# Tokens laid out as 56 rows by 56: the first and last transform as four 64 by 64 products, the row sums on VectorE

## The chip, the cores and the metric

The kernel runs on one core of a Trainium2 chip. The metric is the device time of one launch in microseconds (us), the median of three runs. A profile of one execution is there beside it; its engines are PE (TensorE's products; PEld is its loading of weights), DVE (VectorE), ACT (ScalarE), POOL (GpSimd) and SP (SyncE, which issues nearly all transfers).

## What is computed

The input is 32 images of 56 by 56 places with 96 channels, all float32. The reference, cut to what matters:

```python
def reference(x, ...):
    # layer 0: LayerNorm over channels, 96 -> 192 product (first half used), 3x3 convolution 192 -> 96
    mu, var = mean(x, -1), mean((x - mu)**2, -1)
    h = (x - mu) * rsqrt(var + 1e-5) * ln_w + ln_b
    x1, _ = split(h @ w_in + b_in, 2)
    x = x + silu(conv3x3(x1, conv_w, 'SAME') + conv_b)
    # layer 1, attention part: t is (32, 3136, 96)
    t = x.reshape(32, 3136, 96)
    h = relu(bn1(layernorm(t) @ w1.T))                 # 96 -> 192
    X = fft(h, axis=1, norm='ortho')                   # over the 3136 places
    xr = relu(X.real * rd - X.imag * idg + rb)
    xi = relu(X.imag * rd + X.real * idg + ib)
    y = ifft(xr + 1j * xi, axis=1, norm='ortho').real
    t = t + bn2(y @ w2.T)                              # 192 -> 96
    # layer 1, FFN with float8 (e5m2) operands: 96 -> 384 -> 96
    h = relu(qlinear(layernorm(t), W1, b1))
    return (t + qlinear(h, W2, b2)).reshape(x.shape)
```

## The kernel before

An image's 3136 tokens lie as 112 partitions (`N1`) by 28 columns (`N2`). `Image` holds the tiles of one image, and each step of it is a small function. Along an image the steps are:

- `fetch` loads x in four chunks of up to 8 columns, `take_in` forms LayerNorm's sums with `stats` (bn_stats on DVE, the power -1/2 on POOL, L147) and scales into `xa` (L410).
- `make_image` calls `image`: TensorE transposes and takes the row sums of a Winograd scheme for four output rows at once, by a product with the table `rows6_sb` (tile `im`, L165). ACT copies it to `img` (L167), the only buffer of its kind; `make_seam` copies two columns between its halves (L418, L419).
- `conv` takes 24 products for each of 9 parts (three groups of 32 output channels by three pairs of planes), tile `cv` (L182 for a part's first product, L186 for the rest). Four of them go to four groups of 32 columns of TensorE's array. `conv_sums` and `conv_silu` combine them on DVE to four output rows each (L203), `to_tokens` transposes back (`st`, L219), `conv_end` adds to the tokens (L439).
- The Fourier transform over 3136 = 112 x 28 is done in two stages. `tokens_a` transposes four columns (`tp_n`, L158), `forth` multiplies by w1 (`ph`, L232; relu on ACT, L235), `forth_a` transforms over the 112 rows (`pa<-h,fa_sb`, L241: 112 by 112, moving 384), and `store_a` writes the result to DRAM (`da`).
- `fetch_a` reads `at` back with the other axis on the partitions. `second` forms the second stage in 28 pages p, in units of eight, eight, eight and four (`px`, L256: for u = 0 and 1 the first 128 channels, for u = 2 the last 64, with the unit's two halves of pages in the two column halves of the array). `second_parts` and `second_relus` apply the filter (L261 to L282). `second_w2` multiplies by w2 (`pg`, L295 and L299), `second_back` goes back through the second stage (`pe`, L309), `store_back` writes `de` to DRAM.
- `fetch_y` reads `y`, `back` transforms back over the rows (`py<-y,ia_sb`, L317), `back_end` adds to the tokens (L516) and forms the third LayerNorm's sums.
- `normal` writes the normalised tokens as float8 (L535 on ACT, L539 on DVE, two columns each), `ffn_start` transposes (L156), `ffn_first` multiplies by W1 (`pf`, L328), `ffn_middle` adds the bias, takes relu (L335) and rounds to float8 (`hq`, L336), `ffn_second` multiplies by W2 (`po`, L342), `ffn_end` adds (L351, L352) and `store` writes out.

The order is a plan by hand. `put(when, step, ...)` in `plan(b)` gives each step of image b a time in eighths of an image's period (8 b + when), the steps are sorted by it and issued so; the scheduler of the language then orders each engine's instructions by priority. About three images are in work at once. `in_turn` keeps loads in program order for the first images.

[...]Tile `a` (two buffers of a bank) holds `tp_n` and `pf`, `q` (two) `im`, `cv` and `st`, `c` (two) `ph`, `px` and `py`, and `b` (two) `pa`, `pg`, `pe` and `po`.

## Time and profile before

| | us |
|---|---|
| median of 3 runs | 3040.65 (3039.39 to 3045.61) |
| span of the profiled execution | 3036.8 |
| PE busy | 2978.4 (98%) |
| PEld busy | 2445.3 (81%) |
| DVE busy | 2348.2 (77%) |
| ACT busy | 2277.4 (75%) |
| POOL busy | 647.5 (21%) |
| mean granted TensorE clock | 0.990 of full |
| largest queue of transfers | 349.24 MB, 43.5% of 16 DMA engines |

A profiled span runs from the first to the last instruction; the median includes what lies around it. A row of the profile names line, engine, operation, tiles (`out<-in`), shape, count, busy time and the mean of one, and then the idle time before its instructions with what ended it. In rows of the timeline the first number is the start in us and the second the time to the last end of the merged instructions. An f32 product is shown as two instructions, a float8 one as one.

### The profile page before, as it was taken

The page shows a single profiled execution, that of the slowest core. Times are in us where ns is not written, and L with a number is a line of the kernel's source. Part 1 is how long each engine was busy: PE and PEld are TensorE (multiplying, and loading weights), DVE is VectorE, ACT ScalarE, POOL GpSimd, SP SyncE. Part 2 cuts the span into 40 slices and gives each one's busy share as a digit, 9 for nine tenths or more (in the row PEclk, how much of TensorE's full clock was granted, in tenths as well). Part 3 has the DMA queues.
Part 4 walks back from the last instruction along what each step waited for, and adds up shares of the span by engine and source line. Part 5 has one row for each costly group of instructions (what it writes and reads, how often), then busy time and mean ns, then how long its engine had stood idle before and what let it go on. Part 6 is the DMA issues. An engine that isn't in the chain of part 4 may idle for free.

```text
span 3036.8 us, 84414 instructions
## 1 busy us (share of the span) xinstructions
PE 2978.4 (98%) x32693; PEld 2445.3 (81%) x32693; DVE 2348.2 (77%) x7248; ACT 2277.4 (75%) x5703; POOL 647.5 (21%) x398
## 2 busy tenths in 40 slices
PE   8999999999999999999999999999999999999997
PEld 7678788888888887888888888888888888888775
DVE  5548777888778887778887778887778887777778
ACT  3467777787777787777787777787777877777877
POOL 2202122222112221122221222221222221121111
PEclk9899999999999999999999999999999999999998
DMA  3533444443454444444444444434444434444443
GB/s 85 144 93 94 117 126 124 118 123 98 121 133 126 117 116 108 122 130 122 123 109 114 125 126 123 127 98 122 124 128 122 123 96 124 129 129 104 113 123 78
DMA packets 495435, 355.37 MB, mean 117 GB/s; under 512 B 329992, under 2 KB 459304, under 8 KB 494808
## 3 DMA queue, kind: packets, MB, share of 16 engines
q1 hardware_dynamic: 493146, 349.24, 43.5%
q8 instruction: 257, 4.21, 0.6%
q10 hardware_dynamic: 1888, 0.74, 0.1%
q14 instruction: 144, 1.18, 0.1%
HBM read 195.73 MB, written 154.14 MB: 115 GB/s over the span
## 4 chain that ended last, share of the span: by engine, by line
PE 88%; DMA 5%; DVE 3%; ACT 2%; issue 1%; POOL 0%; SPq 0%; ACTq 0%; DVEq 0%
PE cv L186 14%; PE ph L232 10%; PE px L256 10%; PE pa L241 9%; PE im L165 7%; PE pe L309 6%; PE pg L299 5%; PE py L317 5%; PE pg L295 5%; PE po L342 4%; PE pf L328 4%; PE cv L182 3%; PE st L219 3%; PE tp_n L158 2%; DMA de<-es 2%; DMA xl<-in_x 1%
## 5 line engine op out<-in xcount | busy, mean ns | idle before, releaser
L186 PE MATMUL cv<-img,wv 97*32 97x196 f32 x13248 | 621.6, 331 | 0.0
L147 POOL TENSOR_TENSOR rs_c<-var_c,mhalf 112x8 f32<-112x8 f32 (+1 forms) x128 | 206.7, 1615 | 1894.1 <-DVE var_c L145 879.1
L186 PEld LDWEIGHTS cv<-img,wv 97*32 97x32 f32 x13248 | 426.8, 109 | 106.9
L235 ACT ACTIVATE h<-ph,rs_b 112x192 f32<-112x192 f32 x896 | 340.1, 449 | 74.1 <-PE ph L232 74.0
L232 PE MATMUL ph<-w1a,n2t 97*112 97x192 f32 x1792 | 381.2, 335 | 2.0 <-ACT n2t L225 0.9
L241 PE MATMUL pa<-h,fa_sb 112*112 112x384 f32 x896 | 372.3, 497 | 0.8 <-ACT h L235 0.8
L330 ACT CAST h<-pf 128x448 f16<-128x448 f32 x672 | 367.5, 567 | 1.1 <-PE pf L328 1.0
L256 PEld LDWEIGHTS px<-fb_sb,at 112*64 112x64 f32 (+1 forms) x3584 | 319.2, 166 | 58.1 <-issue 8.7
L256 PE MATMUL px<-fb_sb,at 112*64 112x112 f32 (+3 forms) x3584 | 353.5, 272 | 8.1 <-DMA at<-da 4.0
L165 PE MATMUL im<-rows_sb,xa 112*97 112x168 f32 x1792 | 321.2, 313 | 2.1 <-DVE xa L410 1.4
L232 PEld LDWEIGHTS ph<-w1a,n2t 97*112 97x112 f32 x1792 | 278.5, 177 | 47.4 <-issue 18.1
L147 POOL TENSOR_TENSOR rs_b<-var_b,mhalf 112x8 f32<-112x8 f32 (+1 forms) x128 | 227.7, 1788 | 397.3 <-DVE var_a L145 310.2
L165 PEld LDWEIGHTS im<-rows_sb,xa 112*97 112x97 f32 x1792 | 264.1, 168 | 33.1 <-issue 15.7
L242 ACT COPY u<-pa 112x384 f32<-112x384 f32 x448 | 226.2, 505 | 75.6 <-PE pa L241 75.4
L272 DVE SCALAR_TENSOR_TENSOR sv<-px,spar_sb,av 128x224 f32<-128x224 f32 (+2 forms) x352 | 152.9, 434 | 151.3 <-ACT av L263 149.8
L336 DVE CAST hq<-h 128x448 fp8e5<-128x448 f16 x672 | 256.1, 386 | 7.5
L335 DVE TENSOR_SCALAR h<-h,b1q 128x448 f16<-128x448 f16 x672 | 220.1, 329 | 40.6 <-ACT h L330 36.1
L299 PE MATMUL pg<-w2x,gt 128*112 128x96 f32 (+1 forms) x1792 | 243.1, 258 | 0.0
L167 ACT COPY img<-im 97x336 f32<-97x336 f32 x448 | 205.5, 461 | 48.6 <-PE im L165 25.8
L299 PEld LDWEIGHTS pg<-w2x,gt 128*112 128x112 f32 (+1 forms) x1792 | 240.8, 178 | 0.0
L261 ACT ACTIVATE av<-px,spar_sb 128x224 f32<-128x224 f32 (+2 forms) x352 | 162.8, 462 | 100.9 <-PE px L256 99.1
L295 PE MATMUL pg<-w2y,gt 128*112 128x192 f32 (+1 forms) x896 | 226.8, 335 | 1.1 <-DVE gt L282 0.7
(121 smaller groups left out, 6197.6 us busy)
## 6 DMA issues: line engine op xcount, KB each, us to landing
da<-u SPq DMA_DIRECT2D x224, 336.0 KB, 3.1
at<-da SPq DMA_DIRECT2D x224, 336.0 KB, 4.2
de<-es SPq DMA_DIRECT2D x448, 84.0 KB, 2.0
y<-de SPq DMA_DIRECT2D x224, 168.0 KB, 2.5
out<-t SPq DMA_DIRECT2D x224, 168.0 KB, 2.6
t<-in_x SPq DMA_DIRECT2D x96, 336.0 KB, 4.4
xl<-in_x SPq DMA_DIRECT2D x93, 336.0 KB, 4.5
t<-in_x SPq DMA_DIRECT2D x32, 168.0 KB, 3.8
```

The source lines that it names most:

```text
L147: nc.gpsimd.tensor_tensor(rs, var, mhalf[:, :n], ALU.pow)
L165: nc.tensor.matmul(ps[:, j], xa[:, j, :], rows6_sb, start=True, stop=True)
L186: tc.keep_in_program_order(nc.tensor.matmul(*args, start=(dx == 0), stop=(dx == 2)))
L232: nc.tensor.matmul(ph[:, j, :], n2t[:, 2 * j2 + j, :], w1a, start=True, stop=True)
L235: nc.scalar.activation(h[:, j], ph[:, j], AF.Relu, scale=rs[:, 2 * j2 + j : 2 * j2 + j + 1])
L241: nc.tensor.matmul(pa, fa_sb, h, start=True, stop=True)
L242: nc.scalar.copy(u[:, 2 * j2 : 2 * j2 + 2, :], pa)
L256: nc.tensor.matmul(px[rows, j], lhs, fb_sb[:, first(p) : first(p + 1)], start=True, stop=True)
L295: nc.tensor.matmul(pg[:, :, j, :], lhs, w2y, start=True, stop=False, skip_group_check=True)
L299: nc.tensor.matmul(pg[:, half, j, :], lhs, w2x, start=False, stop=True, skip_group_check=True)
L330: nc.scalar.copy(h1, pf)
L336: nc.vector.tensor_copy(hq[:, k, :], h2, saturate=False)
```

## The change

Tokens lie as 56 rows on 120 partitions (`NQ`): one half of the image's columns on partitions 0 to 55, the other on 64 to 119, with a gap between. The host lays x out so, and gives it a second time with the channels first (`xc`).

- The row sums are formed on DVE from the channel-first copy: the statistics of a whole image give one power on POOL (`scale`), a transpose on TensorE (`turn`), a write to DRAM, and a read back that spreads the factor over the 96 channel partitions (`fetch_r`). `scaled` multiplies, and `differences`, `ends`, `inner` and `outer` form the six planes of `img`. `image`, `make_seam` and `rows6_sb` are gone.
- The Fourier transform is 56 by 56. `transform_a` and `transform_out` each issue four products of at most 64 by 64 places, at two row groups and two column groups of the array, through `together`.
- `pa`, `px`, `pg`, `pe` and `py` share tile `d`, of two banks, in two buffers. `ph` and `po` go to tile `a`. `second` with u = 0 covers up to eight pages, and its u = 1 is gone; the pages of u = 2 are issued in the order of p.
- All columns of `normal` go to ACT; `hq` is rounded once per group of four columns, to columns padded to 128; several work tiles have one buffer (`m`, `sd`, `av`, `sv`, `gw`, `es`).
- `SHIFT` moves the time of nearly every step, `EARLY` and `WRITE` place the row sums ahead of the convolution, and the scheduler's model of the issue queues is shortened (`short_window`).

The diff, cut to its core:

```diff
-N1, N2 = 112, 28
+N2, NT1 = 28, 112
+HP = 64
+BANK = 512
+NQ = HP + HW
+SHIFT = {
+    "back": 0.002, "back:0": -0.012, "back:1": 0.006, "back:3": 0.047, "back:4": 0.02, "back:5": -0.026,
...
+}
-    def image(xa, b, g, t0):
-
-        ps = psq.tile([C + 1, 2, 2, WC * WG], F32, tag="q", name=f"im_{b}_{g}_{t0}")
-        for j in range(2):
-            nc.tensor.matmul(ps[:, j], xa[:, j, :], rows6_sb, start=True, stop=True)
-        j0 = CT * t0 + g + 1
-        nc.scalar.copy(img[:, :, j0 : j0 + CT + 1 : CT].rearrange("c h j k g -> c j h (k g)"), ps)
+    def together(products):
+
+        for i, (to, lhs, rhs) in enumerate(products):
+            if i == 0:
+                nc.tensor.matmul(to, lhs, rhs, start=True, stop=True)
+                continue
+            with tc.high_priority():
+                tc.keep_in_program_order(nc.tensor.matmul(to, lhs, rhs, start=True, stop=True))
-    def transform_a(h, u, b, g, j2):
-
-        pa = psum2.tile([112, 2, H], F32, tag="b", name=f"pa_{b}_{g}_{j2}")
-        nc.tensor.matmul(pa, fa_sb, h, start=True, stop=True)
-        nc.scalar.copy(u[:, 2 * j2 : 2 * j2 + 2, :], pa)
+    def transform_a(h, u, b, g):
+
+        pa = psum2.tile([128, 2, BANK], F32, tag="d", name=f"pa_{b}_{g}")[:, :, : 2 * H]
+        products = []
+        for c in range(2):
+            for r in range(2):
+                rows = slice(HP * r, HP * r + HW)
+                at = h[rows, 2 * c : 2 * c + 2].rearrange("p j c -> p (j c)")
+                products.append((pa[HP * c : HP * (c + 1), r], fa_sb[rows], at))
+        together(products)
+        nc.scalar.copy(u.rearrange("m r j c -> m r (j c)"), pa)
...
-        n = PG if u < 2 else (p1 - p0) // 2
-        px = psum2.tile([128, n, 2, w], F32, tag="c", name=f"px_{b}_{m}_{u}")
-        for j in range(n):
-            for half in range(1 if u < 2 else 2):
-                p = p0 + u * PG + j if u < 2 else p0 + half * n + j
-                rows = slice(0, 128) if u < 2 else slice(64 * half, 64 * half + 64)
-                lhs = ats[p // PG][:, p % PG, :128] if u < 2 else ats[p // PG][:, p % PG, 128:]
-                nc.tensor.matmul(px[rows, j], lhs, fb_sb[:, first(p) : first(p + 1)], start=True, stop=True)
...
+            for p in range(p0, p1):
+                rows = slice(64 * ((p - p0) // half), 64 * ((p - p0) // half) + 64)
+                at = fb_sb[:, first(p) : first(p + 1)].rearrange("n (r k) -> n r k", r=2)
+                nc.tensor.matmul(to[rows, :, (p - p0) % half, :], ats[p // PG][:, p % PG, 128:], at, start=True, stop=True)
...
-        py = psum2.tile([N1, G4, C], F32, tag="c", name=f"py_{b}_{g}")
-        nc.tensor.matmul(py, ia_sb, y, start=True, stop=True)
-        return py
+        n = min(2, NG - 2 * q)
+        ps = psum2.tile([128, 2, G4, BANK // G4], F32, tag="d", name=f"py_{b}_{q}")[:, :n, :, :C]
+        products = []
+        for h in range(2):
+            for r in range(n):
+                rows = slice(HP * r, HP * r + HW + 1)
+                to = ps[HP * h : HP * (h + 1), r].rearrange("p (i j) c -> p i j c", i=2)
+                products.append((to, ia_sb[rows], y[rows, :, h]))
+        together(products)
...
+    def scaled(im, h):
+
+        a = view(im.xc[h], 0, (LINE // 2, 2 * N2), (WG + 1, 2), (1, WG))
+        r = im.rb[h].rearrange("c (j i g) -> c j i g", i=2, g=WG)
+        nc.vector.tensor_tensor(a, a, r, ALU.mult)
+    def inner(im, h, k):
+
+        x = im.xc[h]
+        b, a = (x[:, :, START[i] : START[i] + WG] for i in (2, 3))
+        nc.vector.tensor_tensor(planes(h, k), a, b, ALU.add if k == 1 else ALU.subtract)
...
-            if j < 2:
+            if j < 4:
                 nc.scalar.activation(
...
         def put(when, f, *args):
+            when += sum(SHIFT.get(key, 0) for key in shifts(f.__name__, args))
             order.append((8 * b + when, len(order), lambda: f(im, *args)))
...
-            at = CONV - 2.485 + 0.531 * i
+            at = CONV - EARLY - 0.35 + 0.531 * i
...
+    EARLY, WRITE = 6.2, 3.5
...
+WINDOW = (1, 1, 2)
```

## The prediction

> **What bounds the kernel now.** I read the busy shares first, then the chain that ended last, then the busy times of the steady stretch from 400 to 2600 us (columns there: length, then busy us and instruction count of PE, PEld, DVE, ACT, POOL; granted clock; DMA share; GB/s), and last the timeline of PE for prices.

> ```profile
> PE 2978.4 (98%) x32693; PEld 2445.3 (81%) x32693; DVE 2348.2 (77%) x7248; ACT 2277.4 (75%) x5703; POOL 647.5 (21%) x398
> ...
> PE 88%; DMA 5%; DVE 3%; ACT 2%; issue 1%; POOL 0%; SPq 0%; ACTq 0%; DVEq 0%
> ```

> ```profile
> 400.00:2600.00 2200.00, 2193.42 (x24430) 1808.53 (x24429) 1746.45 (x5387) 1696.44 (x4262) 490.36 (x288) 1.00 0.45 119
> ```

> PE idles 6.6 us in 2200, at full clock: work taken off PE is time, work put on others is not, until they near PE's period. The stretch holds 24 images (672 ACT copies out of ph, 28 per image): **91.7 us per image**, 32 x 91.7 = 2934, so the remaining 103 us of the 3036.8 us span are ramp and tail.

> Busy means of PE overlap (a 384-column product "takes" 497 ns), so I price by the distance between starts:

> ```profile
> 1506.46 0.36 PE L182 MATMUL cv<-img,wv 97*32 97x196 f32 x1
> 1506.47 0.37 PE L186 MATMUL cv<-img,wv 97*32 97x196 f32 x3
> 1506.66 0.33 PE L182 MATMUL cv<-img,wv 97*32 97x196 f32 x1
> ...
> 1508.49 0.33 PE L182 MATMUL cv<-img,wv 97*32 97x196 f32 x1
> ...
> 1510.48 0.33 PE L182 MATMUL cv<-img,wv 97*32 97x196 f32 x1
> ...
> 1515.41 0.60 PE L219 MATMUL st<-ident,s 128*112 128x128 f32 x4
> 1515.94 0.35 PE L182 MATMUL cv<-img,wv 97*32 97x196 f32 x1
> ...
> 1518.07 0.32 PE L219 MATMUL st<-ident,s 128*112 128x128 f32 x1
> ...
> 1547.04 0.99 PE L256 MATMUL px<-fb_sb,at 112*64 112x112 f32 x16
> 1547.96 0.55 PE L328 MATMUL pf<-n3t,w1q 96*128 96x448 fp8e5 x2
> ...
> 1573.98 0.81 PE L241 MATMUL pa<-h,fa_sb 112*112 112x384 f32 x2
> 1574.62 0.35 PE L328 MATMUL pf<-n3t,w1q 96*128 96x448 fp8e5 x1
> 1574.82 0.73 PE L165 MATMUL im<-rows_sb,xa 112*97 112x168 f32 x4
> 1575.39 0.49 PE L219 MATMUL st<-ident,s 128*112 128x128 f32 x3
> ```

> An f32 product is two records (passes): pa 0.64 us for two passes of 384 columns, im 0.57 for four of 168, both 0.83 to 0.85 ns a column. The convolution's 48 records of 196 columns take 1.99 us: 12 steps of 0.166, each as long as one pass alone, so its four 32-column tiles run side by side. A part before which PE was in another mode takes longer: st x4 to cv is 0.53 where four of st elsewhere take 0.44 (0.09 into tiles), cv to st 2.13 where 1.99 is one part (0.14 out of them).

> [...] Here only column groups are seen overlapping; no row groups occur. [...] L182's second pass starts after three L186 first passes, so a tile's waiting pass doesn't stop the other tiles. [...]

> **The change, part by part, us per image.**
> - *im gone*: 56 records x 0.1425 = **-8.0** on PE; its 14 evacuations and two seams leave ACT (205.5 + 21.5 us in the page and by-form rows, /32 = 7.1), the xa scaling leaves DVE (108.9 / 32 = 3.4).
> - *pa as four 64x64*: 14 products x 0.64 = 9.0 become 7 groups of two steps of 0.32 = 4.5: **-4.5**. *py likewise*: 7 x 0.64 = 4.5 become 4 groups, 2.6: **-1.9**. Row groups are unseen; bounds: four at once as taken; two at once, no gain; one at a time, 0.32 x 56 = 17.9 and 0.32 x 28 = 9.0.
> - *Mode changes*: along PE's compiled order I count 21 per image before and 47 after: 13 more round trips x 0.23 = **+3.0**. A change between two tiled modes is not priced anywhere; taken alike.
> - *px of the last 64 channels*: before, its two column halves alternate, and 16 records take 8 steps (0.92 with the way out). After, four pairs' products go to the lower half and then four to the upper. Nothing shows how far a half runs ahead: 0 if the queue reaches past eight passes, +2.7 if halves never overlap (28 more steps x 0.096). I take an overlap of two passes, as cv holds one pass waiting per tile: 6 + 6 + 6 + 2 steps, **+1.9**.
> - *120 rows instead of 112*: 28 transposes x 8 columns x 0.83 ns = +0.2; the added transpose `turn` +0.1. po's stationary goes from 112 to 128 columns: its 84 starts are 51 ns apart for 96 columns, so weights may bind; bounds -0.7 (43 ns) to +0.5; I take **-0.3** since w1q of 128 columns loads in 103 ns, hq of 112 in 134.
> - PE sum: 91.7 - 8.0 - 4.5 - 1.9 + 3.0 + 1.9 + 0.0 = **82.2**.
> - *Row sums on DVE*: 18 instructions, 12,600 elements. xa gives 549 ns for 384 and 950 for 768: 1.04 ns each, and successive rows overlap by about 80 ns, so about 0.06 fixed: 13.1 + 1.1 = +14.2. Off DVE: xa 3.4; xn wholly to ACT (128.5 / 32 = 4.0); one rounding of hq for three (14 fixed parts, 0.9); fused u 0 and 1 (15 fewer, 1.5); s written in runs of 14, not with stride (526 ns now against 386 of the longer L282): 12 x 0.1 = 1.2. DVE 1746.45 / 24 = 72.8 becomes 72.8 + 14.2 - 11.0 = **76**. ACT: 70.7 - 7.1 + xn 5.7 - 3.5 (fewer, longer copies) = **66**. Both lie under 82, so I price them at nothing, covered by PE; DVE's cover is thin (93%). If PE's products came cheaper still, DVE would be next.
> - *Waits*: DVE is in order, and the sums for the next image wait on `img`, still one buffer, until the convolution has read each plane. Behind them queue the px, py and cv readers, for which PE's two d tiles wait. The bufs=1 tiles (m, sd, av, sv, gw, es) couple engines more. PE idles 0.3 us per image now; I take **1** and bound it by 0 and 6.
> - *Queues*: POOL's four powers become one of 28 columns; from 4 columns (1.1 us) to 8 (1.7 to 2.0), about 5 us: POOL idles 79%. SP issues 57 transfers an image for 50: xc (624 KB x2) and rb (602 KB x2) added, rd twice; rb waits for rd to land, and xl, at, y and out queue behind it. The landing of such transfers is 2 to 4.5 us and they are asked for some 60 us early; bytes rise 22%, the DMA share from 0.45 to about 0.55. Hidden.
> - *Ramp*: image 0 needs all four row statistics (done at 15.3 us now), the power 5, the turn and two transfers 8, then about 10 of row sums before the first convolution: 38 to 40 us instead of 27.3, and im's 8 us of ramp work are gone from that gap. Image 1's sums queue on DVE behind image 0's. +18, bounds +5 and +35. The tail moves normalisation from DVE to ACT: 0.

> Sum: 32 x 83.2 + 103 + 18 = 2783 as span. The runs' median is 3040.65, 3.9 above the profiled span: **2787**.

> **Rivals.** (1) Stalls: the order on paper doesn't hold and PE idles 5 to 6 us an image: 2915 to 2950. For it: DVE at 93%, half the buffers. Against: PE idles 0.3 now at DVE 79%. (2) Row groups don't overlap: pa and py back at 9.0 and 4.5, 88.6 + 1 per image, 2990. (3) *Slower*: tile a paces PE. Its two one-bank tiles served tp_n and pf, 35 uses an image; ph, po and turn make it 57. Measured from first product to end of last copy, ph holds its tile 2.2 us, po 2.2, tp_n 1.9, pf 1.7: 57 x 1.9 / 2 = 54 us. ACT is in order, and a late ACT lengthens each hold; from a mean of 3.2 us the period passes 91.7, and at 3.4 it is 97: 3230. The holds would have to grow by 70% on an engine at 80%, which speaks against it. (4) The four products run one after another, the change not doing what it says: 82.2 + 13.4 + 6.4 = 102 an image, 3390; cv's four tiles speak against it.

> **How the numbers follow.** Main case 0.73 (own range 2690 to 2880: px -0 to +2.7, po, ramp, stall 0 to 3), (1) 0.12, (2) 0.05, (3) 0.06, (4) 0.03, no difference 0.01. Faster 0.90, same 0.01, slower 0.09; 0.2%, 6 us, is about what a measurement here can tell from no change. The range reaches to 2960 to take in the stalls, leaving out 0.05 below and 0.14 above.

> **What would show it.** Right: im gone; pa as eight records whose starts lie in two bunches 0.32 apart; pa to the next product about 0.7 us; PE still over 95% busy; DVE near 76 and ACT near 66 us an image; px of 64 columns in about 14 steps. Wrong: pa's eight records over more than 1.2 us; PE under 93% with waits on DVE or ACT at pa, px or ph; DVE above PE.

## The result, and the profile after

| | before | after |
|---|---|---|
| median, us | 3040.0 (3039.2 to 3045.6) | 3334.8 (3328.0 to 3343.7) |
| ratio | | 1.097 (95% interval 1.095 to 1.099) |
| span of the profiled execution | 3036.8 | 3341.9 |
| mean granted TensorE clock | 0.990 | 0.915 |

The change is slower by 9.7%; the forecast was 2787 in a range from 2690 to 2960. The busy shares and the chain that ended last, from the page of the kernel after:

```profile
PE 2972.6 (89%) x32277; PEld 2191.4 (66%) x32277; DVE 2441.8 (73%) x6128; ACT 2156.7 (65%) x4871; POOL 582.7 (17%) x304
...
PE 44%; DVE 19%; DMA 17%; ACT 10%; issue 3%; SPq 2%; POOL 0%; DVEq 0%; ACTq 0%; POOLq 0%
```

No engine took PE's place: all are less busy than before in share. More than half of the chain lies off PE now (44% PE, 88% before). The stretches by time (columns as in the prediction: length, then busy us and count of PE, PEld, DVE, ACT, POOL, then granted clock, DMA share, GB/s), steady part:

```profile
400.00:2800.00 2400.00, 2189.49 (x24115) 1627.54 (x24115) 1800.33 (x4495) 1607.44 (x3643) 432.97 (x216) 0.93 0.52 134
```

That is 24 images at 100.0 us. PE idles 210.5 us of it, **8.8 us per image**, and the clock of 0.93 is made of stretches at full and at half clock only: about 15% of the time at half. Laid out with the trace's clock records, 100.1 us per image (between the first ph products of images 4 and 28, the first image being 0) are 84.4 us of work at full clock, 8.8 idle and **6.9 lost** because 13.8 us of work ran at half clock. "Work" is the time in which PE has any record, with what ran at half clock counted half. Counted the same way, the kernel before takes 91.9 us per image: 91.6 of work, 0.3 idle, nothing lost. DVE takes 75.0 and ACT 67.0 us after the change.

The four 64 by 64 products, in the timeline of PE (start, us to the last end, engine, line, operation, tiles, shape, count):

```profile
1499.32 0.87 PE L275 MATMUL ph<-w1a,n2t 97*120 97x192 f32 x4
1500.12 0.53 PE L283 MATMUL pa<-h,fa_sb 56*64 56x384 f32 x1
1500.12 0.55 PE L286 MATMUL pa<-h,fa_sb 56*64 56x384 f32 x3
1500.49 0.48 PE L283 MATMUL pa<-h,fa_sb 56*64 56x384 f32 x1
1500.50 0.49 PE L286 MATMUL pa<-h,fa_sb 56*64 56x384 f32 x3
1500.92 0.36 PE L416 MATMUL pf<-n3t,w1q 96*128 96x448 fp8e5 x1
```

All four run at once, in two bunches of four passes 0.37 us apart, and 0.80 us lie from the first to the next product (0.81 in the median of 134 such groups at full clock). So the packing works; the time goes elsewhere. Where a stall ahead of pa comes from is seen in the chain of waits between 1491 and 1512 us (start, us, what):

```profile
1491.38 0.57 DVE t L443
1491.97 3.19 DMA out<-t
...
1495.59 0.55 SPq L447
...
1496.24 3.54 DMA rd<-rt
1499.80 4.34 DMA rb<-rd
...
1504.16 1.79 DVE xc L531
...
1508.15 1.78 DVE xc L531
1509.93 0.36 DVE sv L336
...
1510.53 0.36 DVE sv L337
1510.89 0.37 DVE sv L339
...
1511.31 0.53 PE pa L283
```

Read it downwards: SP stands before the t loads (L447) until an `out` store has landed; rd and rb come behind in its queue and take 3.5 and 4.3 us; VectorE stands at xc until rb is there; the readers of px (L336 to L339) come behind it in its order (px was written by 1503.49 and av, which they read too, by 1506.45; the first of them starts at 1509.85), tile d stays held, and PE waits 2.5 us to write pa.

The wait of SP at the head of this chain is its smallest part. What rd writes out is the copy rt, and that was late itself (two rows of the timeline, of PE and of ACT):

```profile
1493.38 0.27 PE L505 MATMUL tr<-ident,rs_a 120*28 120x120 f32 x1
1495.33 0.23 ACT L507 COPY rt<-tr 28x120 f32<-28x120 f32 x1
```

ScalarE came to rt 1.7 us after the turn, and with rt done at 1495.56 SP held rd only 0.7 us longer (0.7 in the median of images 8 to 27, 2.0 at most). From the end of the turn to rb there are 10.5 us, of which rd and rb take 7.9. And the turn waited for nothing here: PE was not idle ahead of it, and the power that it reads had been ready for 194 us (median, about two images). Its place in PE's order sets when the chain begins.

The list of waits gives the chain in sums (who waited for whom: us in all, times, longest):

```profile
DVE xc L531 <- DMA rb<-rd: 96.3, 41, 8.2
...
PE pa L283 <- DVE sv L339: 58.3, 21, 4.7
```

Of the 8.8 us of idle PE per image, 2.3 end at pa with this release and 1.4 at py when y has landed; the rest is spread over pf (1.6), ph (1.2), po (0.8), cv (0.7) and others. The experiments ask whether this chain is the cause, or one of many.

### The profile page after: what moved, and what is told of

Read it like the earlier page. It is cut to its first block, busy times and chain, and to the rows that moved or that the text cites. A ratio compares the mean times of both kernels' runs of the same rounds, so it can differ in the third digit from the quotient of the medians.

```text
span 3341.9 us, 80656 instructions
## 1 busy us (share of the span) xinstructions
PE 2972.6 (89%) x32277; PEld 2191.4 (66%) x32277; DVE 2441.8 (73%) x6128; ACT 2156.7 (65%) x4871; POOL 582.7 (17%) x304
## 4 chain that ended last, share of the span: by engine, by line
PE 44%; DVE 19%; DMA 17%; ACT 10%; issue 3%; SPq 2%; POOL 0%; DVEq 0%; ACTq 0%; POOLq 0%
PE ph L275 6%; PE cv L228 6%; PE pg L380 4%; PE pg L376 4%; PE px L312 4%; DMA de<-es 3%; PE pe L392 3%; DMA rb<-rd 3%; DMA y<-de 3%; PE pa L283 3%; PE px L320 3%; DMA rd<-rt 3%; PE pf L416 3%; DVE xc L531 2%; ACT xn L687 2%
## 5 line engine op out<-in xcount | busy, mean ns | idle before, releaser
L184 POOL TENSOR_TENSOR rs_c<-var_c,mhalf 120x8 f32<-120x8 f32 (+1 forms) x128 | 220.9, 1726 | 1575.6 <-DVE var_c L182 1562.2
L275 PE MATMUL ph<-w1a,n2t 97*120 97x192 f32 x1792 | 423.0, 362 | 43.0 <-ACT y L438 22.5
L277 ACT ACTIVATE h<-ph,rs_b 120x192 f32<-120x192 f32 x896 | 327.1, 419 | 181.8 <-PE ph L275 180.6
L687 ACT ACTIVATE xn<-t,shift,rs_c 120x96 fp8e5<-120x96 f32 x896 | 367.2, 475 | 43.5 <-DVE shift L681 43.5
L275 PEld LDWEIGHTS ph<-w1a,n2t 97*120 97x120 f32 x1792 | 299.4, 197 | 115.3 <-ACT y L438 31.2
L184 POOL TENSOR_TENSOR rs_b<-var_b,mhalf 120x8 f32<-120x8 f32 (+1 forms) x128 | 206.3, 1614 | 758.9 <-DVE var_b L182 742.2
L416 PE MATMUL pf<-n3t,w1q 96*128 96x448 fp8e5 x672 | 253.0, 391 | 50.9 <-ACT n3t L411 25.8
L283 PE MATMUL pa<-h,fa_sb 56*64 56x384 f32 x448 | 216.8, 567 | 58.3 <-DVE sv L339 58.3
L312 PEld LDWEIGHTS px<-fb_sb,at 112*128 112x128 f32 x1792 | 250.4, 211 | 21.8 <-issue 6.8
L312 PE MATMUL px<-fb_sb,at 112*128 112x112 f32 (+1 forms) x1792 | 256.5, 295 | 9.1 <-DMA at<-da 7.5
L286 PE MATMUL pa<-h,fa_sb 56*64 56x384 f32 x1344 | 249.4, 568 | 1.4 <-ACT h L277 1.3
L336 DVE SCALAR_TENSOR_TENSOR sv<-px,spar_sb,av 128x224 f32<-128x224 f32 (+4 forms) x256 | 132.7, 518 | 129.7 <-ACT av L327 129.0
```

The costliest lines, as they stand in the source:

```text
L184: nc.gpsimd.tensor_tensor(rs, var, mhalf[:, :n], ALU.pow)
L275: nc.tensor.matmul(ph[:, j, :], n2t[:, 2 * j2 + j, :], w1a, start=True, stop=True)
L277: nc.scalar.activation(h[:, j], ph[:, j % 2], AF.Relu, scale=rs[:, j : j + 1])
L283: nc.tensor.matmul(to, lhs, rhs, start=True, stop=True)
L286: tc.keep_in_program_order(nc.tensor.matmul(to, lhs, rhs, start=True, stop=True))
L312: nc.tensor.matmul(to[:, (p - p0) // PG, :, p % PG, :], ats[p // PG][:, p % PG, :128], at, start=True, stop=True)
```

## The experiments

All change the kernel after, except e9 and e14, which change the kernel before. The table gives, per image in the steady part, the period and its three parts as worked out above (work at full clock, idle PE, loss by half clock); the ratio is to the kernel before on the same chip. "Rest" is the profiled span less 32 periods: the start and the end of a run, and what its first and last images take more or less than the period.

| | median us | ratio (95%) | period | work | idle | half clock | rest |
|---|---|---|---|---|---|---|---|
| before | 3040 |  | 91.9 | 91.6 | 0.3 | 0 | 96 |
| after | 3335 | 1.095 to 1.099 | 100.1 | 84.4 | 8.8 | 6.9 | 139 |
| e1 rb earlier | 3273 | 1.074 to 1.080 | 96.8 | 84.2 | 7.9 | 4.7 | 171 |
| e2 rb from a fixed source | 3172 | 1.039 to 1.048 | 92.9 | 84.2 | 6.2 | 2.5 | 193 |
| e3 no row sums | 3298 | 1.081 to 1.088 | 96.7 | 83.1 | 7.5 | 6.1 | 207 |
| e4 px halves alternate | 3325 | 1.089 to 1.095 | 99.2 | 83.2 | 9.4 | 6.7 | 150 |
| e5 no shifts | 3321 | 1.087 to 1.095 | 98.4 | 83.7 | 8.6 | 6.0 | 176 |
| e6 default window | 4015 | 1.315 to 1.326 | 121.5 | 89.7 | 15.9 | 15.9 | 117 |
| e7 stores by ACT | 3425 | 1.123 to 1.131 | 101.9 | 85.6 | 8.8 | 7.5 | 152 |
| e8 e1 further, with e4 | 3255 | 1.068 to 1.072 | 97.1 | 82.8 | 6.9 | 7.3 | 147 |
| e9 before without im | 3152 | 1.036 to 1.040 | 96.4 | 85.8 | 7.6 | 3.0 | 64 |
| e10 e3 without its loads | 3115 | 1.024 to 1.028 | 90.5 | 83.4 | 4.4 | 2.6 | 217 |
| e11 e10, double buffers | 3091 | 1.015 to 1.021 | 91.3 | 83.8 | 4.7 | 2.8 | 168 |
| e12 e10, six t | 3023 | 0.992 to 0.996 | 87.3 | 84.6 | 2.0 | 0.7 | 238 |
| e13 five t1 | 3329 | 1.090 to 1.100 | 99.7 | 84.3 | 9.1 | 6.3 | 148 |
| e14 e9, five t1 | 3193 | 1.047 to 1.054 | 98.2 | 85.8 | 8.9 | 3.6 | 53 |
| e15 e8, five t1 | 3243 | 1.064 to 1.072 | 94.8 | 83.8 | 6.7 | 4.3 | 209 |
| e16 more lead | 3210 | 1.055 to 1.059 | 94.8 | 82.9 | 8.7 | 3.2 | 175 |
| e17 no wait for rd, xl | 3188 | 1.048 to 1.053 | 94.5 | 85.2 | 6.0 | 3.3 | 154 |
| e18 e15, t loads apart | 3312 | 1.086 to 1.091 | 98.4 | 83.6 | 7.9 | 7.0 | 161 |

One column hardly moves: in all but e6 and the kernel before, PE's own work is 83 to 86 us. The medians differ by idle time, by its half clock, and by the last column, which is no constant. Without the row sums (e3, e10, e12) the start is longer: the period of image 0 is 112 us in e10 and 70 in the kernel after. That hides a part of what these edits gain per image.

### Is it rb's wait, or the work of the row sums? (e1 to e3)

```diff
+for k, v in (("fetch", -.8), ("take_in", -.8), ("scale", -.8), ("turn", -.8), ("fetch_r", -.8)): SHIFT[k] += v   # e1
-nc.sync.dma_start(im.rb[h], im.rd[h]... .partition_broadcast(C))                                                 # e2
+nc.sync.dma_start(im.rb[h], xc[im.b, h].rearrange("c j l -> c (j l)")[:, : N2 * HW])
-for i, (f, *args) in enumerate(steps): put(...)     # e3: scaled, differences, ends, inner, outer are not put
```

> The next image's chain of loads, statistics, turn and row factors (fetch, take_in, scale, turn, fetch_r) is put 0.8 units (about 10 us) earlier in the order, so that the two rd and two rb transfers come ahead of the t loads that wait for out stores in SP's queue. Theory A (SP's queue: rb comes late, VectorE stands in order at xc L531, the px readers behind it come late, tile d stays held, PE idles and its clock then falls to half): the 96 us that VectorE waited for rb go, most of the 2.4 us per image of idle PE ahead of pa go and so does a part of the 7 us per image of half clock: 94 to 96 us per image, 3150 to 3210 us. Theory B (VectorE's own work, not the wait, holds the px readers): within 15 us of 3335. Theory C (many small waits spread over ScalarE, VectorE and transfers, this one no more than its own 96 us / 32 = 3 us per image): 3260 to 3310.

> rb is read from in_xc (same bytes, no wait for rd), so the row sums are computed with wrong factors; the power, turn and the rd store stay, and rb stays behind the t loads in SP's queue unless the scheduler moves it. Theory A: rd's landing (3.5 of about 11 us) leaves the chain, the rest of the queue stays: 3230 to 3300. Theory B: no change, within 15 us of 3335. Theory C: 3290 to 3320.

> VectorE's 18 row-sum instructions per image are left out (img stays at 0.5); their loads, turn, rd and rb transfers stay. VectorE falls from 75 to about 60 us per image and no longer waits for rb. Theory A: what the wait cost goes and little more: within 30 us of e1. Theory B: VectorE's load is the cause, so clearly more than e1: 2950 to 3080. Theory C: between 3200 and 3260, the remaining waits on ScalarE and transfers untouched.

e1 gave -62 us, theory C's size. rd and rb did come ahead of the t loads in SP's queue, yet VectorE's wait for rb was 119 us, not less than 96. The traces say why. From the issue of rb to `scaled`, its first reader, there are 4.2 us in the kernel after and 4.0 in e1 (medians of images 8 to 27): the compiled order brought `scaled` forward with the transfer, so rb had no more lead than before. Besides, tr now stood until ScalarE had read ph out of tile a, 1.9 us of idle PE per image:

```profile
1449.83 0.26 PE L512 MATMUL tr<-ident,rs_a 120*28 120x120 f32 x1 [1.72 <-ACT h L284]
```

(It did not stand for the power, as e8's expectation takes it: that had been ready for 189 us.)

e2 gave -163, more than any theory said; VectorE's wait for rb fell to 59 us. But more than a wait went. With no rd to wait for, rb was issued 53 us ahead of the turn, and the row sums began 96 us ahead of their image's first cv product, where the kernel after has 49. The 163 us (5%) are what both are worth together.

e3 took 13 us per image of work off VectorE and gave only -37, within 30 us of e1 as theory A has it and far from theory B's 2950 to 3080. In the steady part it is worth more, 3.4 us per image or 108 us in 32, of which the longer start took 68 back. So **VectorE's work is not the main cause** (theory B falls), though it is not free. The idle PE moved to cv and ph, behind conv_end, which waited 101 us for t loads, and behind ScalarE.

### PE's own work, the order and the queue (e4 to e8)

```diff
-for p in range(p0, p1):                                                       # e4, second with u = 2
+for p in [p0 + half * i + j for j in range(half) for i in range(2)]:
+SHIFT = {}                                                                    # e5
-with short_window(), tile.TileContext(...)                                    # e6
+with tile.TileContext(...)
-nc.sync.dma_start(to, u[...]); nc.sync.dma_start(rows[:, half], es[...])      # e7
+nc.scalar.dma_start(to, u[...]); nc.scalar.dma_start(rows[:, half], es[...])
+# e8: as e1 with fetch, take_in, scale -1.1, turn -.7, fetch_r -.75; and e4
```

> Only the order of the products of the last 64 channels changes: lower and upper column half alternate again, as in the kernel before. Start to start px of 64 columns falls from 6.1 to about 4.2 us per image (8 steps for 14). If PE's own work sets the end: -1.9 x 32 = -61, 3275. If PE waits for others anyhow: between 0 and -30, 3305 to 3335.

> The table of small shifts of the steps is emptied; everything else stays. Theory C1 (the stalls come from tile, buffer and queue coupling, whatever the fine order): within 60 us of 3335, with other places of idle PE but again 7 to 10 us of it per image. Theory C2 (the shifts make this order bad on the chip): 3150 to 3230. Theory C3 (the shifts help on the chip as on paper): 3400 to 3500.

> The scheduler's issue windows of PE, VectorE and ScalarE (1, 1, 2) are left at their defaults, so the compiled order may leave the written order further. Theory C1: within 60 us of 3335. Theory C2 (short windows bind each engine to an order that the chip's durations don't fit): 3150 to 3250. Theory C3: 3400 to 3500.

> The stores da<-u and de<-es, 22 of SP's transfers per image, are issued by ScalarE, which has just written u and es, so SP no longer stands before them (536 and 382 us of waiting there). ScalarE pays 22 issues. Theory A in its wide form (SP's in-order queue holds other transfers back, and these make the late starts): y, at and rb land earlier, the idle PE of 8.8 us per image halves, its half clock with it: 3100 to 3200. Theory D (engines' own order and tiles, not SP's queue): within 40 us of 3335, or slower by the issues on ScalarE.

> As e1, but loads and statistics are put 1.1 units earlier and the turn and the factors only 0.7, so that PE doesn't stand before tr for the power (1.9 us per image in e1); the two column halves of px alternate as in e4. Theory A: the waits of DVE for rb, and of PE for rs_a, both go: 3120 to 3200. Theory C: other waits take their place: 3230 to 3280.

e4 is the cleanest look at how little PE's work counts. Sixteen px products of 64 columns, in the timelines of the kernel after and of e4:

```profile
500.25 1.42 PE L320 MATMUL px<-fb_sb,at 112*64 112x112 f32 x16
```

```profile
502.31 0.99 PE L320 MATMUL px<-fb_sb,at 112*64 112x112 f32 x16
```

0.43 us saved in each of three units of eight pages and, taken as half, 0.2 in the unit of four: 1.5 us per image or 48 us in all. The time fell by 10, and idle time rose. e5: the table of shifts does nothing on the chip (theory C1), though the stalls stand elsewhere (cv, py and ph in place of pa and pf). e6: without the short windows the same steps take 680 us more, with 15.9 us of idle PE; the compiled order is worth more than any part of the change. e7: taking 22 stores off SP cost 90 us; SP no longer waited there, but stood longer before `out` (980 us for 544), and 22 issues per image now lie in ACT's order (theory D's slower side). e8 gains 18 more on e1 and lies where theory C put it; `scaled` starts 3.9 us after rb's issue, so again rb has no more lead.

### Does a kernel with less work on PE run faster at all? (e9)

```diff
-for j in range(0, j1 - j0, 2): put(at + 0.08 * j, make_image, i, j)
-put(CONV - 0.078, make_seam)
+nc.gpsimd.memset(img, 0.5)
```

> The kernel before without im: its 56 products of the row sums, their 14 copies out and the seams are left out (img stays at 0.5, so the convolution's numbers mean nothing). PE's work falls by 8.0 to 83.4 us per image, about that of the changed kernel (84), but buffers, tiles, queue and order are those of before. Theory S (slack alone: once PE's work is near 84, the other engines' latencies show in any such kernel): PE idles 4 us or more per image and its clock falls, 2900 to 3100. Theory P (the coupling that the change adds is at fault: two tiles d for four of b and c, single buffers, the longer SP queue, the new order): PE stays over 95% busy at full clock, 32 x 83.4 + 103 - 8: 2760 to 2820.

Theory S, and beyond its range (to 3100): products that take 8.2 us of PE's time per image by their starts were taken away from the **kernel before**, with 5.8 us of ScalarE's work, its tiles, buffers and written order untouched, and it became 112 us slower. Its steady part:

```profile
400.00:2600.00 2200.00, 2025.54 (x22036) 1565.79 (x22040) 1670.37 (x5140) 1485.37 (x3698) 460.44 (x276) 0.97 0.43 114
```

PE idles 174.5 us where it idled 6.6, and has a clock of 0.97 for 1.00. A piece of its chain:

```profile
1544.75 2.35 DMA out<-t
1547.48 6.26 DMA t<-in_x
1553.93 0.70 DVE t L439
1555.20 2.71 PE cv L186 x41
```

So "PE idles 0.3 us now", on which the prediction's stall term leaned, was no property of the buffers or the written order: it went as soon as PE was not full. The compiled order of e9 is another one too, and no run parts the two. PE's work fell by 5.8 us and not by 8.2; a likely reading, not shown, is that a product next to a wait is counted with its whole length, where in a full PE the next one overlaps it (a pass of cv lasts 0.33 us and the steps are 0.166 apart).

### Buffers, loads, and the ring of t tiles (e10 to e15)

```diff
-put(..., fetch_c, h); put(..., fetch_r, h); put(..., turn)        # e10, on e3
-tag="m" (sd, av, sv, gw, es), bufs=1                              # e11, on e10
+tag="m" (sd, av, sv, gw, es), bufs=2
-tc.tile_pool(name="tpool", bufs=4)                                # e12, on e10
+tc.tile_pool(name="tpool", bufs=6)
+self.t[half] = tpool.tile(..., bufs=(4, 5)[half])                 # e13; e14 on e9; e15 on e8
```

> As e3, and the transfers xc, rd and rb and the turn are left out too, so that SP issues 51 transfers per image, as many as before[...]. The base for the next two. Theory A in its wide form (SP's queue): 3000 to 3150. Theory P with tiles and buffers: within 50 us of e3's 3298.

> As e10, with two buffers in place of one for m, sd, av, sv, gw and es. If the single buffers couple the engines (theory P1): over 150 us faster than e10 and PE's idle time at most half of e10's. If not (tiles d, t loads, or the order): within 50 us of e10.

> As e10, with six t tiles for four, so that the t loads no longer wait for out stores of four images ago and don't hold what lies behind them in SP's queue. If that wait is the cause (theory P2; in e3 PE stood 2.9 us per image before cv, which waited for t): over 100 us faster than e10. If not: within 50 us of e10.

> The changed kernel with five tiles t1 (second half of an image's tokens) for four; h2 goes from two buffers to one (VectorE alone writes and reads it) and h1 from three to two to make room. Theory R (the ring of t: an image's second half can be loaded only when the store of the image four before has landed, and conv_end, the q tiles and so PE wait for it): over 60 us faster than 3335. Theory Q (the rb transfers still stand behind t loads that wait for out in SP's queue, which this leaves): the wait of VectorE for rb stays, so 3240 to 3290 in all. If the ring is not a cause: within 30 us of 3335.

> e9 (the kernel before without im, 3152) with five tiles t1 for four; n2t and h2 go from three buffers to two to make room. Theory R: the ring sets e9's period (its chain goes from out<-t through t<-in_x and conv_end to cv), so over 150 us faster: 2850 to 3000. If the ring is not what bounds it: within 50 us of 3152.

> e13 and e8 in one: five tiles t1, the rd and rb transfers ahead of the t loads in SP's queue, px halves alternating. Theories R and Q together: both waits gone, PE idles at most 4 us per image and half clock falls to 3 or less: 88 to 92 us per image, 2950 to 3090. If other waits take their place as before: 3180 to 3255.

Three of these edits took their room from other tiles: e13 and e15 (and e17 and e18, which build on e15) have two h1 for three and one h2 for two, and e14 has two n2t and two h2 for three.

e3 to e10 is the largest single step: leaving out xc, rd, rb and the turn, with no work on VectorE left to wait for them, is worth **182 us**, in the range of theory A's wide form. In the steady part it is 6.3 us per image, against 3.4 for the 18 instructions (e3). Which of the transfers counts isn't parted. The bytes alone are hardly it: e10 moves 113 GB/s for e3's 127, but e2 moved 145 and was faster than e3. e11: single buffers are worth 24 us, all of it at the start, and nothing per image (theory P1 falls). e12: two more t tiles are worth 93 us there, a little less than theory P2 asked (100); VectorE's wait for t loads fell from 99 to 2.5 us:

```profile
400.00:2600.00 2200.00, 2136.35 (x25141) 1587.49 (x25142) 1493.57 (x4047) 1651.74 (x3769) 362.33 (x209) 0.99 0.47 118
```

Its period, 87.3 us with 2.0 idle, is 4.6 us under that of the kernel before; the longer start (rest of 238 us for 96) takes nearly all of it back. So PE's work can be near 84 us without PE idling as in e9.

The gain did not carry over. In the changed kernel (e13) SP's wait for `out` fell from 72 to 7 us and conv_end's for t from 16 to 5, and the time stayed: VectorE waited longer for rb instead (134 us for 96). In e9 (e14) a fifth t1 made it 41 us slower, with 5.7 us of idle PE before cv for 3.1. **Theory R falls**, unless the narrower h1, h2 and n2t ate the gain, which no run tests. e15 gains 12 us on e8: other waits took the place of the two. In its chain the longest piece is a new one, a load for the statistics, at which VectorE stands:

```profile
1554.92 7.56 DMA xl<-in_x
1562.78 0.39 DVE gt L356
1563.21 0.58 PE pg L383 x2
```

Nobody needs these statistics yet. In e15 the sums of an image are done 449 us ahead of its turn (median, nearly five images; 491 in the kernel after), so VectorE, with gt and PE's pg behind it, stands for work that its order has put far too early.

### More lead, fewer waits (e16 to e18)

```diff
+SHIFT: fetch -2.0, take_in -1.5, scale -1.5, turn -1.1, fetch_r -1.15, back:0 +.35; xl bufs=3, h2 bufs=1; e4   # e16
+e15 with rb from in_xc, and take_in of a resident tile: im.xl[i] = still[:, : j1 - j0, :]                       # e17
+e15 with SHIFT load:0 +1.2, load:1 +.6; in_turn(..., early=True) for every t load                               # e18
```

> The changed kernel with px halves alternating, three xl buffers for two as in the kernel before (h2 from two to one makes room), and the transfers that VectorE and PE wait for asked for earlier: fetch 2.0 units, take_in and scale 1.5, turn 1.1, fetch_r 1.15 earlier; the first py of an image 0.35 later. Theory L (each idle stretch begins at an in-order engine that waits for a transfer asked for too late: xl, rb, y): the waits for rb and xl fall under 30 us each, PE idles 3 to 5 us per image with 3 of half clock, 90 to 93 us per image: 3010 to 3110. Theory C (as many other waits take their place): 3180 to 3250.

> e15 without the transfers that VectorE's row sums wait for: rb is read from in_xc with no wait for rd, and the statistics of the next image are taken of a resident tile, so that xl isn't loaded; the numbers of the row sums are therefore wrong. All of VectorE's work stays (75 us per image). Theory L: 87 to 90 us per image, 2900 to 3010. Theory B (VectorE's work itself): as e15, 3200 to 3260. Theory C: 3080 to 3200, with py and pg in their place.

> e15 (3243) with one thing more: the t loads of an image are put where the stores that free their tiles have landed long before (the first half 1.2 and 0.6 units later, all in written order), so that SP doesn't wait for an out store with de, y and rb behind it. Theory Q (that wait at the head of SP's queue feeds the late y and rb): SP's wait out<-t falls from 160 us to under 30, the idle PE from 6.8 to 3 to 5 us per image, 89 to 93 us per image: 3020 to 3140. Theory C (any wait taken away leaves the next one, and the order as a whole has no slack): 3200 to 3260.

In e16 one fetch of y stands ahead of the first py of the same buffer, so part of its numbers are those of a later group; its work is whole. VectorE's wait for xl fell to 29 us, as asked, but for rb only to 80, and PE's wait for y rose from 41 to 108: theory C's range. But theory L was not put to the test for rb: `scaled` starts 4.1 us after rb's issue here too, and the row sums begin 51 us ahead of their first cv product, where the kernel after has 49. e17 is in theory C's range too, not in L's (as in e2, the row sums begin earlier there, 98 us ahead of cv): py, px and ph took over, and its chain shows how:

```profile
1549.62 0.47 DVE t L452
1550.11 4.58 DMA out<-t
...
1555.10 0.55 SPq L456
1555.70 1.08 SPq L660
1556.82 4.33 DMA de<-es
1561.57 3.17 DMA y<-de
1564.79 1.54 PE py L292 x2
```

Here the t load at the head of SP's queue (L456) held `de` and `y`. e18 took exactly this wait away (217 us of SP's time in e15, none in e18) and became 70 us **slower**: VectorE still waited 70 us for rb, 50 for xl, and PE 85 for y. Theory Q falls too, and theory C's range (to 3260) was left on the other side. rb's lead was 4.1 us once more.

## Why the prediction was wrong, point by point

The sum was 32 x 83.2 + 121 = 2783 as span; measured 3342. The terms of the difference, per image:

| term | predicted | measured | difference |
|---|---|---|---|
| PE's own work | 82.2 | 84.4 | +2.2 |
| idle PE ("waits") | 1 (0 to 6) | 8.8 | +7.8 |
| half clock | not priced | 6.9 | +6.9 |
| ramp and tail, once | 121 | 139 | +18 |

(2.2 + 7.8 + 6.9) x 32 + 18 = 559, the whole of it.

- *im, pa, py, mode changes, px, po*: right as a sum to 2.2 us in 82, and the 2.2 need not be theirs: in e9, where none of them changed, the work came out at 85.8 and not at 91.6 - 8.2 = 83.4. The packed products overlap as taken, 0.80 us with the way in and out where 0.64 + 0.23 were priced. px's order costs 1.5 us for 1.9 (e4).
- *DVE 76, ACT 66 us*: measured 75.0 and 67.0. "Covered by PE" was right for their busy time and wrong for what it was meant to say: 2.3 us of idle PE per image end with VectorE's release of tile d, at 75 us of work in 100. The work itself was worth 3.4 us per image (e3).
- **The step that failed is "Waits": taking 1 us because "PE idles 0.3 us per image now".** The changed kernel idles 8.8. e9 shows that the 0.3 could not be carried over: the same kernel idles 7.6 us once im's products are gone. The bound of 6 was too low as well, and the clock that falls after idling was left out (6.9 us), though the trace of before shows it at both ends (0.93 in the first 120 us, of which PE idles 20.3, and 0.85 from 2936 to 3036 us, of which it idles 19.4).
- **The second is "Queues ... hidden".** The DMA share of 0.55 was right (0.52), the verdict wrong. "Asked for some 60 us early" was never read from a view. In the written order turn stands at -0.67 units before the row sums' start and the first `scaled` at -0.27, and 0.4 units are 5 us; in the trace `scaled` starts 10.9 us after the turn (median), and rd and rb land one after the other in that time (3.5 + 4.3 above). The five edits that were to lengthen the lead (e1, e8, e15, e16, e18) shortened it to 6.8 to 8.2 us, since `scaled` moved along.
- *Ramp*: the first ph product comes at 98.7 us for 59.7, more than its bound of +35.
- *Rival 1* (stalls of 5 to 6 us) was the right mechanism with too low a price and without the clock. *Rivals 2 and 4* fall with the timeline of pa. *Rival 3* falls as a pace: tile a's 57 uses hold it for 106 us per image of the 200 that two tiles have (ph 2.1 us each, pf 1.8, po 2.0), as estimated. Single waits for it there are: about 2 us of idle PE per image end when ScalarE has read a ph, pf or po.
- *What would show it wrong* said "PE under 93% with waits on DVE or ACT at pa, px or ph": it came so (91.2% in the steady part), only that a rival on the slower side wasn't built from it.

What is shown: the loss is idle time of PE (8.8 us per image for 0.3) and the half clock that follows it (6.9 for 0). VectorE's row-sum work, the shifts, the single buffers, the four t1 tiles and the t loads in SP's queue are each not its cause alone. The transfers of the row sums are its largest named part (182 us from e3 to e10), and a row-sum chain that begins some 47 us earlier without rd took away 163 (e2).

What stays open is why other waits so often took the place of one that had gone. A part of it is seen: where a transfer was moved, its reader moved with it in the compiled order, and rb kept its 4 us through five edits. A reading that fits this, and was not tested, is that the scheduler goes by an estimate of time of its own and puts a reader where the transfer should just have landed. It would also fit that statistics run five images ahead. A general want of lead is not what the traces show: from the issue of y to its py there are 24 us in the median, but 3.2 at the first of each image, where PE waits. An order that holds `scaled` back while rb is asked for earlier would be the test.

Each edit also changes the compiled order of everything, so small differences between two of these kernels, below some 30 us as a rough guess, should not be read as the edit's own effect. No version that keeps the whole computation beat the kernel before; e15 comes nearest (3243).

## What to carry to other kernels

A bound engine's idle time of zero says nothing of what the others will do once it is no longer the bound: before pricing work off the bound engine at its full worth, take that work out of the *old* kernel in one run (here: +112 us where -256 was priced). Price idle TensorE with its clock: in the kernel after and the changed kernels a microsecond of it cost 1.4 (e12) to 2.1 (e8), idle time and half clock taken together. For each new transfer, read its lead (issue to first use) from the compiled order and set it against its landing time, rather than the share of bandwidth (here 4.2 us for rb in the median, where the landing shown took 4.3, at a DMA share of 0.52); and after an edit that is to lengthen a lead, read it again. And compare the steady part beside the total: a longer start can hide a gain per image.

## What was not expected of the hardware

The granted clock is full or half, nothing between (in the kernel after, 78 stretches of each), and half-clock stretches last 3.41 us or a multiple of it (between 400 and 2600 us of the kernel after: 49 stretches, 11 of one unit and 33 of two).

| idle PE in the window, us | after | all 19 |
|---|---|---|
| under 0.8 | 0 of 499 | 1 of 10191 |
| 0.8 to 1.2 | 1 of 38 | 35 of 700 |
| 1.2 to 1.7 | 20 of 29 | 225 of 399 |
| over 1.7 | 33 of 33 | 513 of 517 |

The way back is harder: after a window at half clock with no idle time at all, 54 of 69 returned to full; with any idle time, none of 34 (all 19: 752 of 1093, and 23 of 441). So idle time cost more where it was bunched. A wait of 2 us within one window costs, as an estimate from this table and the one or two units that most stretches last, about 4 to 5: itself, and half of the 3.4 to 6.8 us after it. Waits that left a window under 0.8 us of idle time cost only themselves (1 of 10191 such windows was followed by half clock), which fits e9: 7.6 us idle, only 3.0 lost to the clock.

The first passes of other tiles start ahead of a tile's second pass also when tiles differ in rows (pa's bunches above: four first passes together, the four second passes 0.37 us later), as those of cv's column tiles did in the kernel before (three first passes of L186 at 1506.47, the second pass of L182 at 1506.66).
